# Three placements changed in a gated-scan, linear-attention and fp8 feed-forward kernel: a chunk's norm at the start, group norm's sums in the middle, relu and rounding at the end

## The chip, the cores and the metric

The kernel runs on one core of a Trainium2 chip. The metric is device time in microseconds (us) for one execution, taken as the median of several. The five engines of the core are TensorE (PE, with its weight loads shown apart as PEld), VectorE (DVE), ScalarE (ACT), GpSimd (POOL) and SyncE (SP), which here only issues DMAs. The whole kernel is ordered by hand ("manual schedule"): the order in which the source emits instructions for an engine is the order in which that engine is given them, and engines meet at semaphores.

## The reference

Four images of 64 x 64 pixels with 96 channels go through two layers. Cut to what matters:

```python
# layer 0: x = x + conv(gn(x)); gn is a group norm over 32 groups of 3 channels, per image
xn = layernorm(gn(x)) * gamma + beta                  # per pixel
proj = xn @ W_in + b_in                               # value u, gate g, delta d, and A, B, C (96 x 16 each)
# over the 4096 pixels of an image, one after the other:
h = d * (A * h) + d * (B * u)
y = sigmoid(g) * sum(C * h, axis=states)
x = x + (y @ W_out + b_out)
# layer 1
t = t + attn(ln(t))     # linear attention (no softmax), so K^T V can be folded into one matrix per image
t = t + ffn(ln(t))      # two linear layers, inputs and weights rounded to fp8 (5 exponent bits, 2 mantissa bits),
                        # results rounded to fp16, relu between them
```

The recurrence over pixels is one scan instruction of VectorE per tile. Group norm needs the mean and variance of a whole image before its first pixel can be normed, so the kernel computes them for image b+1 while it scans image b.

## The kernel before

Each image is cut into 8 chunks of 512 pixels, each chunk into 12 tiles (4 groups of states by 3 groups of channels). A tile is one **step**; there are 384 steps. In every step each of the three projections takes three matmuls of 512 columns, and the loop over steps emits, in this order:

```python
for s in range(min(steps), START):      # START = 6; steps 0 to 5 of the scan are planned apart
    call(s)
for s in range(START, K):               # K = 384
    tiles[s + 3].b_proj(); tiles[s + 3].b_copy()      # PE -> bank B (one bank), ACT copies it out
    tiles[s + 1].a_proj()                             # PE -> bank A (two banks)
    tiles[s].c_proj()                                 # PE -> bank C or D
    tiles[s - 1].keep()                               # ACT
    tiles[s + 2].b_mul()                              # POOL
    if tiles[s - 1].on_pool: tiles[s - 1].c_mul_pool()
    tiles[s].scan()                                   # DVE
    tiles[s + 1].a_mul()                              # DVE
    if not tiles[s].on_pool: tiles[s].c_mul()         # DVE
    call(s)                                           # everything else that a table puts at this step
    if tiles[s].on_pool: tiles[s].c_copy()            # ACT
```

`call(s)` emits what the table `AT` puts at step s. Numbers are relative to the first step of a chunk:

```python
AT = {
    "load_x": -39, "centre": -25, "scale": -24, "stats": -22, "rstd": -22, "apply": -21,
    "transpose": -14, "affine": -13, "upper": -13, "low": -12, ...
    "stats_f": 26, "rstd_f": 27, "apply_f": 29, "transpose_f": 30, "quant_in": 31, ...
    "sums": -31,
}
```

The norm of a chunk ahead of its projections is the class `Front`: `centre` and `scale` (POOL, two passes over 128 x 384), `stats` (DVE), `rstd` (POOL, four small operations) and `apply` (ACT, writes tile z), then transposes and projections. The first two chunks are normed in a planned start of their own. For the third chunk (first step 24) the table gives centre -1, scale 0, stats 2, rstd 2, apply 3: all below START, so the first of the two loops above emits all of them at once, after the planned work and ahead of step 6.

Group norm's sums of the next image, one call per chunk of that image:

```python
def sums(self, n):
    self.transpose(n, "M", "gx")                       # PE: four transposes into a bank of ring M (three banks)
    for k, fn in enumerate((AF.Identity, AF.Square)):  # ACT: two passes, each adding up along its rows
        nc.scalar.activation(self.ps, self.ps, fn, bias=self.c if k == 0 else 0.0,
                             accum_out=self.s[:, k, n : n + 1])
...
when = [s0 + AT["sums"] + NT * n for n in range(NCH)]  # one call in 12 steps
if b == 1:
    when = [8, 15, 22, 29, 36, 43, 50, 57]             # the second image: one in 7 steps
```

After the last step a planner orders what is left: feed-forward work of the last three chunks of image 2 and of all eight of image 3. It takes jobs with an engine, an estimated cost and predecessors, and searches orders at random (`end.tries`):

```python
def round_hidden(m):  nc.scalar.copy(v["h16"][:, m, :], v["h", m])              # PSUM -> fp16, 128 x 512
def relu_vector(m):   nc.vector.tensor_scalar(h, h, b1_q[:, m : m + 1], 0.0, ALU.add, ALU.max)
def quant():          nc.scalar.activation(v["hq"], v["h16"], AF.Copy, saturate=False)   # fp16 -> fp8, 128 x 1536
...
for m in range(NK):                                                             # NK = 3
    h = job("PE", 0.24, hidden, m, ...)
    c = job("ACT", 0.57, round_hidden, m, ...)
    r.append(job("DVE", 0.5, relu_vector, m, after=[c]))
a = job("ACT", 1.5, quant, after=r, ...)
a = job("PE", 0.5, project_out, after=[a], ...)
```

Of the kernel before, what the change touches and what calls it, by code (L numbers as in the profile page):

```python
# [13 lines left out]
AF = mybir.ActivationFunctionType  # L14
ALU = mybir.AluOpType
# [24 lines left out]
AT = {  # L40

    "load_x": -39, "centre": -25, "scale": -24, "stats": -22, "rstd": -22, "apply": -21,
    "transpose": -14, "affine": -13, "upper": -13, "low": -12, "proj_d": -9, "d_out": -9,
    "proj_u": -9, "du_out": -9, "write": -9, "read": -6, "proj_gate": -3, "gate_out": -1,

    "gather1": 7, "gather2": 11, "gather3": 14,

    "state_sum": 18, "gated": 18, "project_out": 19, "residual": 19, "stats_a": 20,
# [5 lines left out]
    "hidden2": 38, "relu2": 38, "project_f": 40, "round_out": 40, "bias_out": 40, "total": 46,  # L54
    "store": 51,

    "sums": -31,
}
ON_POOL = (0, 2, 7, 8)
XBUFS = 15  # L60
# [3 lines left out]
def conv_attn_hybrid_kernel(  # L64
# [19 lines left out]
    nc = tc.nc  # L84
# [21 lines left out]
    def sb(tag, shape, dtype, name):  # L106
        pool = big if tag in ("x", "gx", "z", "rep") else work
        return pool.tile(shape, dtype, tag=tag, name=name, bufs=BUFS[tag])
# [123 lines left out]
    b1_q = const.tile([P, NK], F32, name="b1_q")  # L232
# [294 lines left out]
    def at(step, fn, *args):  # L527
        steps.setdefault(step, []).append((fn, args))
# [4 lines left out]
    class GroupNorm:  # L533
# [34 lines left out]

        def sums(self, n):
            self.transpose(n, "M", "gx")  # L570
            for k, fn in enumerate((AF.Identity, AF.Square)):
                nc.scalar.activation(
                    self.ps, self.ps, fn, bias=self.c if k == 0 else 0.0,
                    accum_out=self.s[:, k, n : n + 1],
                )
# [51 lines left out]
    def group_norm(b, s0):  # L627
        q = {}

        def make():  # L630
            q["g"] = GroupNorm(b)
            q["g"].first()

        def call(name, *args):
            getattr(q["g"], name)(*args)

        when = [s0 + AT["sums"] + NT * n for n in range(NCH)]
        if b == 1:  # L640
            when = [8, 15, 22, 29, 36, 43, 50, 57]
        if b > 1:
            at(when[0] - 7, load_gx, b, 0)
        at(when[0] - 2, make)
        for n in range(NCH):
            if n:
                at(max(when[n] - 7, when[n - 1]), load_gx, b, n)
            at(when[n], call, "sums", n)
        for n, name in ((1, "moments"), (2, "mean"), (4, "root"), (6, "diagonal"), (8, "spread"),
                        (8, "spread_out")):  # L650
            at(when[-1] + n, call, name)


    split, rep, gate = {}, {}, {}
# [104 lines left out]
    def front(b, i, s0, f=None):  # L759
        if f is None:  # L760
            f = Front(b, i)
            plan = [
                ("centre", f.centre, nc.gpsimd), ("scale", f.scale, nc.gpsimd), ("stats", f.stats),
                ("rstd", f.ln.rstd), ("apply", f.apply), ("transpose", f.transpose),
                ("affine", f.affine), ("upper", f.upper), ("low", f.low), ("proj_d", f.proj, 2),
                ("d_out", f.d_out), ("proj_u", f.proj, 0), ("du_out", f.du_out),
                ("write", f.write), ("read", f.read),
            ]
            if (b, i) not in xt:
                plan.insert(0, ("load_x", load_x, b, i))  # L770
        else:
            plan = []
        plan += [("proj_gate", f.proj, 1), ("gate_out", f.gate_out)]
        for name, fn, *args in plan:
            at(s0 + AT[name], fn, *args)

    state = {}
    chs = {}
# [86 lines left out]
    def state_sum(g, last=None, first=None):  # L865
# [5 lines left out]
        for cg in range(NCG):  # L871
# [10 lines left out]
    end = Plan(  # L882
        {"A": 2, "B": 1, "C": 1, "M": 3, "yg": 1, "xal": 2, "xat": 1, "xn8": 2, "bu": 5, "h": 3, "rep": 2,
         "xs": 2, "xl": 2, "z": 2, "mv": 4},
        {"ACT": 0.5, "DVE": 2.5, "POOL": 1.5},
    )
    end.last = {}
    end.tries = 800

    def place(plan, s0):  # L890

# [161 lines left out]
    def ffn(b, i, s0):  # L1053
        nm = f"{b}_{i}"
        v, ln = {}, LayerNorm(1e-5, f"f_{nm}")
# [56 lines left out]
                v["h16"] = sb("rep", [P, NK, TC], F16, f"h16_{nm}")  # L1112
            nc.scalar.copy(v["h16"][:, m, :], v["h", m])  # L1113

        def relu_vector(m):
            h = v["h16"][:, m, :]
            nc.vector.tensor_scalar(h, h, b1_q[:, m : m + 1], 0.0, ALU.add, ALU.max)  # L1117

        def quant():
            v["hq"] = sb("bu", [P, NK, TC], F8, f"hq_{nm}")  # L1120
            nc.scalar.activation(v["hq"], v["h16"], AF.Copy, saturate=False)  # L1121

        def project_out():
            ps = v["ps"] = bank("A" if phase["end"] else "M", [P, J, C], f"y2_ps_{nm}")
# [56 lines left out]
        def job(engine, cost, fn, *args, **kw):  # L1181
            return None if fn in done else end.job(engine, cost, fn, *args, **kw)

        a = job("SP", 0.5, fetch, after=[end.last.get((b, i))], late=2.5, take=[f"xal:{nm}"])
        a = job("PE", 0.46, attention, after=[a, b == B - 1 and end.last["r"]], take=[f"A:a{nm}"],
                free=[f"xal:{nm}"])
        a = job("DVE", 0.57, residual, after=[a], free=[f"A:a{nm}"])
        a = job("DVE", 1.6, ln.stats, t, after=[a], take=[f"mv:{nm}"])
        a = job("POOL", 1.3 if vector else 1.8, ln.rstd, not vector, after=[a])
        a = job("DVE" if vector else "ACT", 1.9 if vector else 1.8, apply, after=[a], take=[f"xn8:{nm}"], free=[f"mv:{nm}"])  # L1190
        a = job("PE", 0.45, transpose, after=[a], take=[f"C:{nm}"], free=[f"xn8:{nm}"])
        a = job("ACT", 0.6, quant_in, after=[a], take=[f"h:{nm}"], free=[f"C:{nm}"])
        if hidden not in done:
            r, h, c = [], None, None
            for m in range(NK):
                h = job("PE", 0.24, hidden, m, after=[a, h], take=[f"M:{m}{nm}"],
                        free=[f"h:{nm}"] if m == 2 else [])
                c = job("ACT", 0.57, round_hidden, m, after=[h, c],
                        take=[f"rep:{nm}"] if m == 0 else [], free=[f"M:{m}{nm}"])
                r.append(job("DVE", 0.5, relu_vector, m, after=[c]))  # L1200
            a = job("ACT", 1.5, quant, after=r, take=[f"bu:q{nm}"], free=[f"rep:{nm}"])
        a = job("PE", 0.5, project_out, after=[a], take=[f"A:y{nm}"], free=[f"bu:q{nm}"])
        a = job(*(("ACT", 0.48) if vector else ("DVE", 0.56)), round_out, after=[a],
                take=[f"xs:{nm}"], free=[f"A:y{nm}"])
        last_two = b == B - 1 and i > NCH - 3
        a = job(*(("DVE", 0.6) if last_two else ("POOL", 0.95)), bias_out, after=[a], take=[f"xl:{nm}"], free=[f"xs:{nm}"])
        a = job(*(("DVE", 0.8) if last_two else ("POOL", 0.92)), total, after=[a], take=[f"z:{nm}"], free=[f"xl:{nm}"])
# [4 lines left out]
    START = 6  # L1212
# [153 lines left out]
    for b in range(B):  # L1366
        for i in range(NCH):
            g = b * NCH + i
            s0 = g * NT
            if g:  # L1370
                front(b, i, s0, second if g == 1 else None)
            for sh in range(1, NSH):
                if g < N - 1 or sh == 1:
                    at(s0 + AT[f"gather{sh}"], gather, g, sh)
            at(s0 + NT, tail, b, i)
            s = s0 + NCH * NT
            first = min(24, AT["fetch"])
            at(s + first if b == B - 1 else min(s + first, K - 4), ffn, b, i, s)
        if b + 1 < B:
            group_norm(b + 1, b * NCH * NT)  # L1380
        s = (b + 1) * NCH * NT
        at(s if s == K else s + AT["gram_add"] - NT + 1, attn_matrix, b, s)
# [82 lines left out]
```

## Time and profile before

| | before |
|---|---|
| time, median of 3 | 1202.92 us (1202.42 to 1204.29) |
| span of the profiled execution | 1199.1 us |
| busy PE / PEld | 1148.7 us (96%) / 876.9 us (73%) |
| busy DVE | 1110.0 us (93%) |
| busy POOL | 1032.2 us (86%) |
| busy ACT | 817.8 us (68%) |
| DMA | mean 152 GB/s |

Rows such as `L824 DVE TENSOR_TENSOR_SCAN h<-Aps,state,bu` name the source line, the engine, the operation and the tiles that it writes and reads. In a timeline each row begins with its start and its duration in us, and a bracket at the end tells how long the engine had been idle before it and which instruction ended that idle time. Lines that matter here: L269 is every projection matmul (told apart by the bank it writes: Bps, Aps, Cps, Dps), L805 is `b_copy`, L808 `b_mul`, L817 `a_mul`, L824 `scan`, L396 `apply` on ACT (tile z in layer 0's norm, xn ahead of the feed-forward), L543 the transposes of group norm's sums, L572 the sums, L910 the gating that follows a chunk's sum over states, L920 the residual after layer 0's output projection (o_ps), L1085 the transposes of xn, L1113 `round_hidden`, L1117 `relu_vector`, L1121 `quant`, L403 `apply` on DVE, L1142 and L1149 the last two additions of the feed-forward.

The ends of matmuls are modelled, so two matmuls in a row overlap on the page; their starts tell the rate. In the stretch from 803 to 837 us the 512-column projections start 0.23 us apart.

### The profile page before, as it was taken

The page shows a single profiled execution, that of the slowest core. Times are in us where ns is not written, and L with a number is a line of the kernel's source. Part 1 is how long each engine was busy: PE and PEld are TensorE (multiplying, and loading weights), DVE is VectorE, ACT ScalarE, POOL GpSimd, SP SyncE. Part 2 cuts the span into 40 slices and gives each one's busy share as a digit, 9 for nine tenths or more (in the row PEclk, how much of TensorE's full clock was granted, in tenths as well). Part 3 has the DMA queues.
Part 4 walks back from the last instruction along what each step waited for, and adds up shares of the span by engine and source line. Part 5 has one row for each costly group of instructions (what it writes and reads, how often), then busy time and mean ns, then how long its engine had stood idle before and what let it go on. Part 6 is the DMA issues. An engine that isn't in the chain of part 4 may idle for free. (4 is left out here: it accounts for less than half of the span.)

```text
span 1199.1 us, 19211 instructions
## 1 busy us (share of the span) xinstructions
PE 1148.7 (96%) x5899; PEld 876.9 (73%) x5899; DVE 1110.0 (93%) x2091; ACT 817.8 (68%) x1828; POOL 1032.2 (86%) x1178
## 2 busy tenths in 40 slices
PE   7799999999999999999999999999999999999885
PEld 6567777677777777777777777777777777777663
DVE  6789999999999999999999999999999999999865
ACT  5465666565555777777777777777777777776476
POOL 3877888888988898999998899999999999988564
PEclk8989999999999999999999999999999999999987
DMA  7566776877776766776677677677776787667221
GB/s 187 127 127 145 153 162 159 175 156 160 168 162 150 162 156 146 175 175 156 155 158 164 152 176 177 135 160 160 163 174 153 163 181 159 151 146 165 60 74 46
DMA packets 104288, 182.12 MB, mean 152 GB/s; under 512 B 42637, under 2 KB 50769, under 8 KB 104186
## 3 DMA queue, kind: packets, MB, share of 16 engines
q1 hardware_dynamic: 90060, 106.96, 37.0%
q0 software_dynamic: 13536, 73.93, 31.0%
q8 instruction: 46, 0.75, 0.3%
q14 instruction: 56, 0.46, 0.1%
q10 hardware_dynamic: 590, 0.02, 0.0%
HBM read 69.12 MB, written 24.77 MB: 78 GB/s over the span
## 5 line engine op out<-in xcount | busy, mean ns | idle before, releaser
L808 POOL TENSOR_TENSOR bu<-bu,rep 128x512 f32<-128x512 f32 x384 | 512.3, 1342 | 53.6 <-ACT state L834 38.5
L824 DVE TENSOR_TENSOR_SCAN h<-Aps,state,bu 128x512 f32<-128x512 f32 x336 | 426.0, 1268 | 0.6 <-POOL ch L857 0.5
L805 ACT ACTIVATE bu<-Bps,b_bac 128x512 f32<-128x512 f32 x384 | 262.3, 683 | 188.7 <-PE Bps L269 185.9
L817 DVE SCALAR_TENSOR_TENSOR Aps<-Aps,b_bac,rep 128x512 f32<-128x512 f32 x384 | 281.8, 734 | 12.6 <-PE Aps L269 12.6
L269 PE MATMUL Bps<-xs,w 128*128 128x512 f32 x768 | 268.5, 431 | 16.1 <-ACT bu L805 15.6
L269 PE MATMUL Aps<-xs,w 128*128 128x512 f32 x768 | 242.4, 396 | 1.2 <-DVE h L824 1.1
L857 POOL TENSOR_TENSOR ch<-ch,h 128x512 f32<-128x512 f32 x128 | 172.5, 1348 | 14.1 <-ACT ch L854 10.7
L269 PEld LDWEIGHTS Aps<-xs,w 128*128 128x128 f32 x768 | 143.6, 188 | 38.0 <-DVE h L824 3.7
L269 PEld LDWEIGHTS Bps<-xs,w 128*128 128x128 f32 x768 | 126.5, 191 | 61.1 <-ACT bu L805 26.3
L269 PE MATMUL Aps<-xl,w 128*128 128x512 f32 x384 | 151.9, 396 | 0.0
L269 PE MATMUL Bps<-xl,w 128*128 128x512 f32 x384 | 151.8, 395 | 0.0
L269 PE MATMUL Dps<-xs,w 128*128 128x512 f32 x384 | 121.0, 396 | 0.0
L269 PE MATMUL Cps<-xs,w 128*128 128x512 f32 x384 | 120.7, 395 | 0.3 <-ACT ch L854 0.3
L848 DVE SCALAR_TENSOR_TENSOR ch<-Dps,b_bac,h 128x512 f32<-128x512 f32 x160 | 118.6, 741 | 0.8 <-PE Dps L269 0.7
L863 POOL DMA_DIRECT2D ch<-ch x94 | 90.1, 958 | 0.8 <-DMA ch<-ch 0.8
L269 PEld LDWEIGHTS Bps<-xl,w 128*128 128x128 f32 x384 | 72.5, 189 | 17.7
L269 PEld LDWEIGHTS Dps<-xs,w 128*128 128x128 f32 x384 | 72.3, 188 | 17.6
L269 PEld LDWEIGHTS Aps<-xl,w 128*128 128x128 f32 x384 | 72.2, 188 | 17.7
L269 PEld LDWEIGHTS Cps<-xs,w 128*128 128x128 f32 x384 | 71.9, 188 | 17.9 <-ACT ch L854 0.4
L854 ACT ACTIVATE ch<-Cps,b_bac 128x512 f32<-128x512 f32 x96 | 65.8, 685 | 22.9 <-PE Cps L269 22.9
L269 PE MATMUL Dps<-xl,w 128*128 128x512 f32 x192 | 75.8, 395 | 0.0
L269 PE MATMUL Cps<-xl,w 128*128 128x512 f32 x192 | 75.7, 394 | 0.0
(200 smaller groups left out, 2048.2 us busy)
## 6 DMA issues: line engine op xcount, KB each, us to landing
ch<-ch POOLq DMA_DIRECT2D x94, 768.0 KB, 6.6
rep<-ddd SPq DMA_DIRECT2D x124, 384.0 KB, 7.0
ddd<-dd SPq DMA_DIRECT2D x31, 384.0 KB, 3.2
xl<-lo SPq DMA_DIRECT2D x62, 128.0 KB, 2.5
x<-in_x_dram SPq DMA_DIRECT2D x32, 192.0 KB, 2.9
xatd<-xat SPq DMA_DIRECT2D x32, 192.0 KB, 3.6
xal<-xatd SPq DMA_DIRECT2D x32, 192.0 KB, 2.9
out_dram<-o SPq DMA_DIRECT2D x32, 192.0 KB, 2.1
```

Source lines behind the costliest of these rows:

```text
L269: nc.tensor.matmul(ps, lhsT=wt[:, n], rhs=mv, start=(n == 0), stop=(n == 2))
L805: nc.scalar.activation(self.bu, self.b_ps, AF.Identity, bias=self.bias(0))
L808: nc.gpsimd.tensor_tensor(self.bu, self.bu, rep[self.b, self.i][:, 1, self.cg], ALU.mult)
L817: nc.vector.scalar_tensor_tensor(self.a_ps, self.a_ps, self.bias(1), rep[self.b, self.i][:, 0, self.cg], ALU.add, ALU.mult,)
L824: nc.vector.tensor_tensor_scan(self.h, self.a_ps, self.bu, 0.0 if self.i == 0 else state[self.sh, self.cg], ALU.mult, ALU.add,)
L848: nc.vector.scalar_tensor_tensor(self.slot(), self.c_ps, self.bias(2), self.h, ALU.add, ALU.mult)
L854: nc.scalar.activation(self.ch, self.c_ps, AF.Identity, bias=self.bias(2))
L857: nc.gpsimd.tensor_tensor(self.ch, self.ch, self.h, ALU.mult)
L863: nc.gpsimd.dma_start(chs[g, 0], chs.pop((g, sh)), accum_op=ALU.add)
```

## The change

It has three parts. First, the third chunk's norm is not emitted ahead of step 6 but spread over steps 6 to 9. Second, group norm's sums are split: the transposes stay where they were, ACT's two passes come one step later. Third, in the planned end, GpSimd takes the relu of one of three row blocks in chunks of odd number, and the rounding to fp8 in chunks whose number is divisible by four; the random search gets more tries.

```diff
-    "sums": -31,
+    "sums": -31, "sums_out": -30,

         def sums(self, n):
             self.transpose(n, "M", "gx")
+
+        def sums_out(self, n):
             for k, fn in enumerate((AF.Identity, AF.Square)):

             at(when[n], call, "sums", n)
+            at(when[n] + AT["sums_out"] - AT["sums"], call, "sums_out", n)

         plan += [("proj_gate", f.proj, 1), ("gate_out", f.gate_out)]
+        late = {"centre": 0, "scale": 0, "stats": 1, "rstd": 2, "apply": 3}
         for name, fn, *args in plan:
-            at(s0 + AT[name], fn, *args)
+            step = s0 + AT[name]
+            at(max(step, START + late[name]) if name in late else step, fn, *args)

-    end.tries = 800
+    end.tries = 1500

-        def relu_vector(m):
+        def relu_rounded(m, engine):
             h = v["h16"][:, m, :]
-            nc.vector.tensor_scalar(h, h, b1_q[:, m : m + 1], 0.0, ALU.add, ALU.max)
+            engine.tensor_scalar(h, h, b1_q[:, m : m + 1], 0.0, ALU.add, ALU.max)

         def quant():
             v["hq"] = sb("bu", [P, NK, TC], F8, f"hq_{nm}")
-            nc.scalar.activation(v["hq"], v["h16"], AF.Copy, saturate=False)
+            if i % 4:
+                nc.scalar.activation(v["hq"], v["h16"], AF.Copy, saturate=False)
+            else:
+                nc.gpsimd.tensor_copy(v["hq"], v["h16"], saturate=False)

-            r, h, c = [], None, None
+            r, h, c, on_pool = [], None, None, (1,) if i % 2 else ()
             ...
-                r.append(job("DVE", 0.5, relu_vector, m, after=[c]))
-            a = job("ACT", 1.5, quant, after=r, ...)
+                r.append(job(*(("POOL", 1.0) if m in on_pool else ("DVE", 0.45)), relu_rounded, m,
+                             nc.gpsimd if m in on_pool else nc.vector, after=[c]))
+            a = job(*(("ACT", 1.5) if i % 4 else ("POOL", 2.2)), quant, after=r, ...)
```

## The prediction

> **What bounds the kernel now.** I read four views in this order: busy shares over the span, the table of waits, the timelines of the places that the waits point to, and the busy time of the last 75 us.
>
> The shares over forty slices come first: PE 9 almost throughout, DVE 9, ACT 5 to 7, and two weak ends.
>
> ```profile
> PE   7799999999999999999999999999999999999885
> DVE  6789999999999999999999999999999999999865
> ACT  5465666565555777777777777777777777776476
> ```
>
> ACT has slack, so in the middle an operation of ACT matters only if somebody stands behind it. The table of waits says where that is:
>
> ```profile
> ACT gx_ps L572 <- PE gx_ps L543: 25.3, 23, 1.8
> PEld Bps L269 <- ACT bu L805: 26.3, 24, 7.7
> ```
>
> Group norm's sums keep ACT standing 23 times, 1.1 us each, and PE waits for the copy-out of bank B, once for 7.7 us. That one is in the start; the timeline of 47 to 66 us has it:
>
> ```profile
> 59.46 1.54 ACT L396 ACTIVATE z<-z,nmr_c,rstd_c 128x96 f32<-128x96 f32 x4 [8.13 <-POOL nmr_c L384]
> 56.47 0.74 DVE L371 BATCH_NORM_STATS2 st_c<-z 128x6 f32<-128x96 f32 x4 [3.33 <-POOL z L670]
> 64.59 0.76 DVE L817 SCALAR_TENSOR_TENSOR Aps<-Aps,b_bac,rep 128x512 f32<-128x512 f32 x1 [3.58 <-PE Aps L269]
> 61.63 1.22 PE L269 MATMUL Bps<-xs,w 128*128 128x512 f32 x2 [7.44 <-ACT bu L805]
> ```
>
> ACT stands 8.13 us at the third chunk's apply, whose mean and rstd POOL gives only at 59.4. The copy-out behind it is late, bank B is full, PE stops for 7.44 us, and DVE has gaps of 3.33 and 3.58.
>
> For the middle I lay a chunk with sums beside one of the last image, which has the same feed-forward work but no sums:
>
> ```profile
> 423.75 0.65 ACT L572 ACTIVATE gx_ps<-gx_ps,gmc 96x512 f32<-96x512 f32 x1 [1.14 <-PE gx_ps L543]
> 425.14 1.53 ACT L396 ACTIVATE xn<-x,nmr_f,rstd_f 128x96 fp8e5<-128x96 f32 x4
> 425.65 1.30 PE L1085 MATMUL xq_ps<-ident,xn 128*128 128x128 fp8e5 x4
> 428.03 0.69 DVE L910 TENSOR_TENSOR yg<-y_ps,gate 96x512 f32<-96x512 f32 x1 [0.90 <-PE y_ps L872]
> ```
>
> ```profile
> 808.75 1.54 ACT L396 ACTIVATE xn<-x,nmr_f,rstd_f 128x96 fp8e5<-128x96 f32 x4
> 811.39 0.40 PE L1085 MATMUL xq_ps<-ident,xn 128*128 128x128 fp8e5 x4
> 813.30 0.68 DVE L910 TENSOR_TENSOR yg<-y_ps,gate 96x512 f32<-96x512 f32 x1
> ```
>
> With sums, xn is pushed behind them on ACT; PE reaches its transposes at 425.65 and takes 1.30 us for them instead of 0.40, as each waits for a slice of xn. Everything after them on PE is late, and DVE stands 0.90 us ahead of the gating. From one L910 to the next it is 34.87 us in chunks with sums (428.03 to 462.89, 534.71 to 569.59) and 33.48 without (813.30 to 846.78).
>
> The end is ACT's (columns: stretch, length, busy and instructions, clock, DMA):
>
> ```profile
> 1140.00:1186.00 46.00, 38.24 (x70) 0.89 0.23 64
> L1121 ACT ACTIVATE hq<-h 128x1536 fp8e5<-128x1536 f16 x11 | 16.0, 1494 | 0.1
> 1178.22 2.93 DVE L403 TENSOR_SCALAR xn<-x,mv_f,rstd_f 128x96 fp8e5<-128x96 f32 x4
> ```
>
> It is 83% busy between 1140 and 1186, and eleven roundings to fp8 at 1.494 us are 16 us of it.
>
> **What the Trainium skill says.** "Perfetto Trace Analysis", Tensor Engine Instruction: ACT, DVE and GpSimd queues are strictly first in, first out. The trace agrees: a finished bank B stood behind an apply that waited 8.13 us. "GPSIMD Engine Reference", Engine selection: with two inputs GpSimd is about half as fast as VectorE, with one roughly at line rate. The first half shows (128x512 with two inputs, L808, 1342 ns); for one input the trace has only small ones, a cast of 128x128 to fp8 at 289 ns and memsets of 128 and 512 elements at 205 and 520 ns. "SBUF — State Buffer", Who interferes with whom: a VectorE tensor_scalar in a two-port mode and a GpSimd operation lock each other out. That fits the last row above: four L403 take 2.93 us while POOL runs L1142 and L1149 without a break, and 1.04 us elsewhere (1154.72).
>
> **Part 1, the third chunk's norm.** Nothing is removed; five calls move behind steps 6 to 9. I followed the new order with durations from the trace. POOL is busy until 54.34 either way (low parts of the weights). Then, before: centre, scale, 1.14 idle, rstd, and b_mul of tile 8 at 59.38. After: b_mul of tile 8 at once, centre and scale (to 57.6), b_mul of tile 9, a gather's issue (0.9), b_mul of tile 10 and c_mul of tile 7, then rstd, done near 64.1. ACT's apply follows at 64.1 to 65.6, the first sums (now in the same step) to 67.1, the copy-out of tile 13 to 67.8. So PE stops again, for the projection of tile 14, until 67.8. In the profile before, that projection began at 74.11: 6.3 us earlier. DVE agrees: a_mul of tile 12 needs a projection that ends near 69.2, so scan 12 starts near 70.7 where it was 77.16, 6.5 us earlier; from there both orders are the same and DVE has no gap over 0.5 us until 88. I take **6.4 us**. POOL would allow 5.3 us in that stretch (its idle times 1.14, 1.01, 0.15, 1.28 and 1.82 vanish), but it has two tiles of lead on the scan.
>
> **Part 2, the sums.** Of the eleven chunks from 388.85 to 740.08 with sums and feed-forward, ten show the full loss of 34.87 - 33.48 = 1.39 us; the first shows a third. With the passes a step later, xn follows at once on ACT (from 422.6), ends near 424.1, and PE's transposes no longer wait. The passes run when ACT otherwise stands (2.76 us idle ahead of the copy-out at 813.72, against 1.5 us for the passes). What stays is the transposes' own time: next matmul 0.35 us after them, and PE is the bound here. Gain 1.39 - 0.35 = 1.04 us, times 10, plus 0.3: **10.7 us**. The chunks without feed-forward (228 to 356 us) run at 31.7 with sums; DVE's own work fills the step there, so nothing. The second image's sums, one in 7 steps: those at 88.37 and 107.19 are followed by PE gaps of 1.45 and 1.53, and a step later they miss apply and share with less: about 2 us back. But the seventh now falls on the step of d_out and apply, the place of the one at 88.37, and the eighth on apply_a: about 1.1 and 0.8 us lost. Net 0.3.
>
> **Part 3, the end.** ACT loses two of eleven roundings, 2 x 1.49 = 3.0 us; DVE loses six relus of about 0.35, off the path. On POOL a one-input pass is an estimate: from 289 ns for 128 elements and (520 - 205)/384 = 0.82 ns for each further one, 0.6 us for a relu and 1.5 us for a rounding, 4 and 3 or more in sum, into 29.9 of 53.1 us busy. ACT is busy 80% of the time from 1140 to the last addition, so 3.0 x 0.8 = 2.4; I take off 0.4 for VectorE operations that meet GpSimd's. A new random order adds spread, not a mean: **2.0 us**.
>
> Sum: 6.4 + 10.7 + 0.3 + 2.0 = 19.4. From 1202.9 that is **1183.5 us**, 1.6% faster.
>
> **Rivals.** (a) The moved norm just moves the stop: rstd stays behind POOL's b_muls, ACT stands at apply as long as before, and PE stops at tile 14 instead of tile 10. For it: ACT still has one apply that waits for POOL. Against it: the stop is met after three more tiles. It would leave 2 us of part 1: 1188. (b) The gain per chunk is the whole 1.39 us or more, if the transposes' 0.35 us hides: DVE waits 0.49 us at L920 in chunks without sums, for PE, which speaks against; 1180. (c) Bank M is held a step longer and PE waits for it. The ring of three next needs that bank at the first h matmul or o_ps, near 815 in the chunk without sums, when the passes have ended near 812.5; I hold it unlikely. It would eat part 2: 1193. (d) In the end GpSimd's roundings lock VectorE out, or the new order is worse on the chip than in its plan: the end gets 2 us longer, 1187. It can also turn out 5 us shorter, 1180.
>
> **Range and chances.** I give part 1 plus or minus 2, part 2 plus or minus 2.5, the second image's sums plus or minus 1.5, the end plus or minus 3; in quadrature 4.7, with both tails of the rivals 1177 to 1190.5 for 8 in 10. A gain of over 2% needs 1178.9, 4.6 us more than my sum: 0.15. Slower by 2% would need a stop that nothing shows: 0.01.
>
> **What would show it.** Right: no PE gap over 4 us between 50 and 70 us, and scan 12 near 70.7; waits of ACT L572 for gx_ps near zero; L1085 at 0.4 us in every chunk; L910 to L910 at 33.8 where it was 34.87; new PE gaps near 1 us at the second image's seventh and eighth sums; last addition 2 us nearer to the last step. Wrong: a stop of 6 us or more near 64 us (rival a), 34.9 unchanged with waits for ring M (c), ACT idle more than before after 1140 while DVE rows stretch beside GpSimd's (d).

## The result and the profile after

| | before | after |
|---|---|---|
| time, median | 1202.67 us (1202.33 to 1204.29) | 1184.09 us (1180.64 to 1186.38) |
| ratio to before, 95% interval | | 0.984 (0.9815 to 0.9866) |
| span of the profiled execution | 1199.1 us | 1182.5 us |

Predicted were 1183.5 us, so the sum holds. The question is whether its terms do. The shares over forty slices of the kernel after come first, the rows that were shown of before:

```profile
PE   7999999999999999999999999999999999999985
DVE  6889999899999999999999999999999999999875
ACT  5556656556556777777877787777777777776475
```

PE's second slice (30 to 59 us) went from 7 to 9: the long stop is out of it. The table of waits of after (total, times, longest):

```profile
ACT bu L811 <- PE Bps L269: 194.4, 171, 2.9
...
PEld Bps L269 <- ACT bu L811: 15.0, 19, 2.8
PEld Bps L269 <- ACT gx_ps L574: 12.6, 15, 0.8
```

The row of ACT standing at the sums for their transposes (25.3 us before) is gone. Lines have moved by a few in the kernel after: L811 is `b_copy`, L814 `b_mul`, L823 `a_mul`, L830 the scan, L854 VectorE's `c_mul`, L863 GpSimd's, L860 `c_copy`, L574 the sums, L916 the gating, L1091 the transposes of xn, L1123 the relu, L1128 and L1130 the rounding on ACT and on GpSimd. PE's longest wait for the copy-out of bank B is 2.8 us where it was 7.7. The last row looks like a new wait for the sums, but isn't: the weight-load unit is idle for 0.84 us each time because PE streams six matmuls of y_ps meanwhile (419.18 to 420.24 in the chunk below), and the sums only happen to end then; before, the same 0.8 us stood under another name. The start's timeline, rows of ACT, PE and DVE:

```profile
63.66 1.54 ACT L396 ACTIVATE z<-z,nmr_c,rstd_c 128x96 f32<-128x96 f32 x4 [4.09 <-POOL nmr_c L384]
63.39 0.51 PE L269 MATMUL Dps<-xl,w 128*128 128x512 f32 x1 [2.76 <-DMA w<-w]
63.93 0.75 DVE L854 SCALAR_TENSOR_TENSOR ch<-Dps,b_bac,h 128x512 f32<-128x512 f32 x1 [2.13 <-PE Dps L269]
67.55 0.76 DVE L823 SCALAR_TENSOR_TENSOR Aps<-Aps,b_bac,rep 128x512 f32<-128x512 f32 x1 [1.74 <-PE Aps L269]
```

ACT stands 4.09 us at the third chunk's apply instead of 8.13. PE still stops, for 2.76 us, but at something the prediction does not have: half a weight that arrives by DMA. A chunk of the middle, with sums, after:

```profile
415.77 1.54 ACT L396 ACTIVATE xn<-x,nmr_f,rstd_f 128x96 fp8e5<-128x96 f32 x4
418.32 0.65 ACT L574 ACTIVATE gx_ps<-gx_ps,gmc 96x512 f32<-96x512 f32 x1
418.86 0.40 PE L1091 MATMUL xq_ps<-ident,xn 128*128 128x128 fp8e5 x4
420.33 0.69 DVE L916 TENSOR_TENSOR yg<-y_ps,gate 96x512 f32<-96x512 f32 x1
```

xn goes ahead of the sums, PE takes 0.40 us for the transposes instead of 1.30, and DVE no longer stands ahead of the gating. From one L916 to the next it is 33.8 to 34.2 us in seven of these eleven chunks (33.3 to 35.7 in the others). The end, first the 46 us that correspond to those shown of before (columns: stretch, length, busy and instructions of PE, PEld, DVE, ACT, POOL, then clock, DMA share, GB/s), then the relus and roundings (count: shortest, median, longest in ns), then VectorE beside GpSimd:

```profile
1124.00:1170.00 46.00, 38.12 (x264) 27.91 (x260) 35.42 (x121) 36.09 (x68) 37.49 (x46) 0.81 0.23 65
```

```profile
L1123 DVE TENSOR_SCALAR h<-h,b_q x27: 340/348/1416, 1116.2 to 1169.0; 128x512 f16<-128x512 f16 x27
L1128 ACT ACTIVATE hq<-h x9: 1467/1483/1502, 1122.0 to 1171.3; 128x1536 fp8e5<-128x1536 f16 x9
L1123 POOL TENSOR_SCALAR h<-h,b_q x6: 2003/2018/2382, 1113.6 to 1167.5; 128x512 f16<-128x512 f16 x6
L1130 POOL CAST hq<-h x2: 1472/1564/1655, 1146.5 to 1164.9; 128x1536 fp8e5<-128x1536 f16 x2
```

```profile
1145.81 3.72 DVE L403 TENSOR_SCALAR xn<-x,mv_f,rstd_f 128x96 fp8e5<-128x96 f32 x4
```

ACT is 2.15 us less busy than before (38.24 to 36.09). A rounding on GpSimd takes 1.5 us, as estimated; a relu takes 2.0 us, not 0.6.

To place the gain, I number the scans by step and compare the time between scans of the two kernels (start of a scan to start of a later scan, from the timelines):

| steps | before | after | gain | predicted |
|---|---|---|---|---|
| start to scan 4 | 46.09 | 45.30 | 0.8 | 0, the same instructions |
| 4 to 12 | 31.07 | 26.18 | 4.9 | 6.4 (first part) |
| 12 to 17 | 13.30 | 13.31 | 0.0 | 0 |
| 17 to 48 | 86.13 | 83.37 | 2.8 | 2 (second image's sums) |
| 48 to 60 | 33.92 | 35.09 | -1.2 | -1.9 (its seventh and eighth) |
| 60 to 66 | 17.74 | 19.18 | -1.4 | 0 |
| 66 to 120 | 144.85 | 144.82 | 0.0 | 0 |
| 120 to 383 | 752.03 | 741.98 | 10.1 | 10.7 (sums, chunks with feed-forward) |
| scan 383 to the end | 73.97 | 73.27 | 0.7 | 2.0 (third part) |

The gains add up to 16.6 us, the difference of the two profiled spans; the medians differ by 18.6. So some 2 us of this table belong to the two executions and not to the kernels. Which rows those are was the first thing to find out.

### The profile page after: what moved, and what is told of

The parts are those of the page before. It is cut to its first block, busy times and chain, and to the rows that moved or that the text cites. A ratio compares the mean times of both kernels' runs of the same rounds, so it can differ in the third digit from the quotient of the medians.

```text
span 1182.5 us, 19167 instructions
## 1 busy us (share of the span) xinstructions
PE 1141.2 (97%) x5884; PEld 874.5 (74%) x5884; DVE 1110.0 (94%) x2085; ACT 816.7 (69%) x1826; POOL 1047.2 (89%) x1186
## 5 line engine op out<-in xcount | busy, mean ns | idle before, releaser
L814 POOL TENSOR_TENSOR bu<-bu,rep 128x512 f32<-128x512 f32 x384 | 513.4, 1346 | 44.6 <-ACT state L840 31.8
L830 DVE TENSOR_TENSOR_SCAN h<-Aps,state,bu 128x512 f32<-128x512 f32 x336 | 426.0, 1268 | 0.7 <-POOL ch L863 0.6
L811 ACT ACTIVATE bu<-Bps,b_bac 128x512 f32<-128x512 f32 x384 | 263.0, 685 | 198.4 <-PE Bps L269 194.4
L823 DVE SCALAR_TENSOR_TENSOR Aps<-Aps,b_bac,rep 128x512 f32<-128x512 f32 x384 | 281.8, 734 | 9.3 <-PE Aps L269 9.3
L863 POOL TENSOR_TENSOR ch<-ch,h 128x512 f32<-128x512 f32 x128 | 173.3, 1354 | 8.9 <-ACT ch L860 4.8
L854 DVE SCALAR_TENSOR_TENSOR ch<-Dps,b_bac,h 128x512 f32<-128x512 f32 x160 | 118.6, 741 | 3.0 <-PE Dps L269 2.8
L860 ACT ACTIVATE ch<-Cps,b_bac 128x512 f32<-128x512 f32 x96 | 66.0, 687 | 24.5 <-PE Cps L269 24.5
```

Source lines behind the costliest of these rows:

```text
L811: nc.scalar.activation(self.bu, self.b_ps, AF.Identity, bias=self.bias(0))
L814: nc.gpsimd.tensor_tensor(self.bu, self.bu, rep[self.b, self.i][:, 1, self.cg], ALU.mult)
L823: nc.vector.scalar_tensor_tensor(self.a_ps, self.a_ps, self.bias(1), rep[self.b, self.i][:, 0, self.cg], ALU.add, ALU.mult,)
L830: nc.vector.tensor_tensor_scan(self.h, self.a_ps, self.bu, 0.0 if self.i == 0 else state[self.sh, self.cg], ALU.mult, ALU.add,)
L854: nc.vector.scalar_tensor_tensor(self.slot(), self.c_ps, self.bias(2), self.h, ALU.add, ALU.mult)
L860: nc.scalar.activation(self.ch, self.c_ps, AF.Identity, bias=self.bias(2))
```

## The experiments

Theory: three independent gains, the first cut short by the DMA and the half clock that follows it, the third by GpSimd's slow relu. Rivals: the parts need each other; the order of the sums matters and not their step; the end's gain is that of another random order.

### Each part alone

```diff
# p1_norm: before, with
+        late = {"centre": 0, "scale": 0, "stats": 1, "rstd": 2, "apply": 3}
-            at(s0 + AT[name], fn, *args)
+            step = s0 + AT[name]
+            at(max(step, START + late[name]) if name in late else step, fn, *args)
# p2_sums: before, with
+    "sums_out": -30,
+        def sums_out(self, n):                 # the two passes, out of sums()
+            at(when[n] + AT["sums_out"] - AT["sums"], call, "sums_out", n)
# p3_end: before, with
-    end.tries = 800
+    end.tries = 1500
+    # relu m = 1 of odd chunks and the rounding of chunks divisible by 4: job("POOL", ...)
```

> The kernel before with the first part alone (third chunk's norm behind steps 6 to 9). The prediction's sum: 6.4 us shorter than before. My reading of the trace after the change: 4.9, because PE's stop no longer ends at ACT's copy-out but at a weight DMA that lands near 63 us. If that is so, this kernel too shows a PE gap of 2 to 3 us near 63 us that ends at a DMA, ACT stands about 4 us at the third chunk's apply, and scan 12 starts 4.9 us earlier relative to scan 4 than before. If instead the 1.5 us are lost because the third chunk's norm and the sums' later pass meet on ACT (rival), this kernel alone gets the whole 6.4.

> The kernel before with the second part alone (sums' two passes a step later). My reading: 10 to 10.5 us shorter than before (ratio near 0.991), all of it in the eleven chunks with sums and feed-forward (34.9 to about 33.9 us per chunk); second image's steps 17 to 66 net within 0.5 us of before; the start's stop of 7.4 us stays whole. Rival: the gain needs the shifted phase that part one brings, then it is under 8 us.

> The kernel before with the third part alone (GpSimd's relus and roundings in the planned end). Prediction: 2.0 us shorter; the trace after shows 0.7 from the last scan to the last addition. I expect 0.5 to 1 us shorter (ratio 0.999 to 1.000), with GpSimd's relu at 2.0 us each and its rounding near 1.5 us. If the prediction's 0.6 us for a relu were a matter of neighbours in the trace after, the relus would be shorter here.

| | time | ratio to before (95%) | in us | steps 4 to 12 | 17 to 48 | 120 to 383 | 383 to end |
|---|---|---|---|---|---|---|---|
| p1_norm | 1197.01 | 0.9958 (0.9942 to 0.9974) | -5.1 | 27.93 | 86.14 | 752.11 | 73.39 |
| p2_sums | 1190.31 | 0.9900 (0.9882 to 0.9917) | -12.0 | 30.72 | 83.36 | 741.88 | 73.31 |
| p3_end | 1199.69 | 0.9975 (0.9966 to 0.9984) | -3.0 | 30.51 | 86.15 | 752.12 | 70.89 |

(In us: the ratio's distance from 1, times 1202.93, the median of before beside these runs.) Together 20.1 us, where all three at once give 19.2 (0.016 x 1202.93; interval 16.1 to 22.3): within the intervals the parts add up. Each part works in its own stretch and leaves those of the others alone, as the columns show. p2_sums puts 10.1 us into the chunks with feed-forward and 2.8 into steps 17 to 48, without the first part's shift. p3_end shows 3.1 us in the end, four times what I had read from the trace after. p1_norm has the expected stop at a DMA, but longer, 4.04 us and not 2 to 3, and gains only 2.6 to 3.1 us between scans 4 and 12, not the 4.9 that I expected of it:

```profile
65.46 0.80 PE L269 MATMUL Dps<-xl,w 128*128 128x512 f32 x1 [4.04 <-DMA w<-w]
66.05 1.05 PE L269 MATMUL dug_ps<-xs,w_dug 128*96 128x512 f32 x2
```

The second row is the hint to the next finding: two matmuls in 1.05 us, where relu_dve below shows the same two in 0.63.

### Executions of the same instructions, side by side

Six of the kernels have the start of after, instruction for instruction (after, and relu_dve, image2, no_pool, round800 and no_pool800 below). Between scans 4 and 12 they took 26.18, 24.96, 26.31, 27.05, 26.14 and 27.33 us. The clock of PE in after (first fence) and in relu_dve (second), in two stretches of 1 us after the DMA stop, reads like this:

```profile
64.00:65.00 1.00, 1.00 (x4) 0.75 (x3) 1.00 (x2) 1.00 (x4) 1.00 (x2) 0.52 1.11 227
65.00:66.00 1.00, 1.00 (x3) 0.74 (x3) 0.81 (x1) 0.97 (x4) 1.00 (x1) 0.50 1.14 233
```

```profile
64.60:65.60 1.00, 1.00 (x6) 0.80 (x5) 1.00 (x2) 1.00 (x4) 1.00 (x2) 1.00 0.99 203
65.60:66.60 1.00, 1.00 (x6) 0.81 (x5) 0.80 (x1) 0.97 (x4) 1.00 (x1) 1.00 1.11 227
```

PE is busy throughout in both; in after it does three or four matmuls per us, in relu_dve six, since the granted clock (third number from the end) is 0.50 in one and 1.00 in the other. In both a stop of PE went ahead, of 2.76 and 2.74 us:

```profile
63.39 0.51 PE L269 MATMUL Dps<-xl,w 128*128 128x512 f32 x1 [2.76 <-DMA w<-w]
63.73 0.79 PE L269 MATMUL dug_ps<-xs,w_dug 128*96 128x512 f32 x2
```

```profile
63.98 0.50 PE L269 MATMUL Dps<-xl,w 128*128 128x512 f32 x1 [2.74 <-DMA w<-w]
64.31 0.63 PE L269 MATMUL dug_ps<-xs,w_dug 128*96 128x512 f32 x2
```

Read us by us, the clock of every run is 1.00 or 0.50, and what a stretch of half clock loses (one minus the clock, summed) comes as 1.7 us or a multiple, so in units of 3.4 us of half clock. The start after PE's stop has none in relu_dve (24.96 us), one in after, image2 and round800 (26.18, 26.31, 26.14), two in no_pool and no_pool800 (27.05, 27.33): about 1.2 us each. The Trainium skill, "TensorE: Matmul & The Clock Gate", Part 1: The HAM clock gate, describes this: an activity monitor halves the matmul clock after an idle window of about 3.4 us that runs freely, so that its phase differs from run to run. The halves and the length agree with the trace. The size of the gap doesn't: here half clock followed stops shorter than the window, of 2.76 to 2.93 us in these starts, and in read_last (below) of 0.61 and 1.65 us around four transposes that took 1.39 us. Step 65 shows best that it need not follow, where every one of the fourteen profiled executions has a PE stop of 2.35 to 2.81 us: five of them had no half clock and took 3.79 to 3.81 us for the step (before and p1_norm among them), nine had it and took 4.57 to 5.36 (p3_end, whose instructions there are those of before, and after). So the row "60 to 66: -1.4" of the table is no effect of the change.

The start of before has half clock too, which has to be kept in mind when its 31.07 us are the measure. From the end of its stop of 7.44 us, at 61.63, to 66.5 us its clock is 0.50. The last pair of matmuls before that ends, and the first after it:

```profile
65.64 1.05 PE L269 MATMUL Bps<-xs,w 128*128 128x512 f32 x2
66.77 0.62 PE L269 MATMUL Aps<-xs,w 128*128 128x512 f32 x2
```

p3_end, with the same instructions, and p2_sums have half clock behind that stop as well (30.51 and 30.72 us). No execution shows the start of before at full clock.

### The order of the sums or their step: same_step

```diff
-            at(when[n] + AT["sums_out"] - AT["sums"], call, "sums_out", n)
+            at(when[n] - 1, lambda n=n: at(when[n], call, "sums_out", n))   # same step, emitted last in it
```

> The kernel after, but the sums' two passes stay in the step of their transposes and are only put behind everything else that the table has for that step (so behind xn on ACT). Theory: what counts in the chunks with feed-forward is that xn goes ahead of the passes, not the step itself; these chunks keep their gain of about 1 us each and this kernel is within 2 us of after, with the second image's steps 17 to 66 about as before. Rival: the passes need the later step, because PE's transposes for them are not done; then ACT stands at the passes again and some 5 to 10 us of the gain are lost.

1185.23 us, ratio to before 0.9856 (0.9841 to 0.987). Steps 120 to 383 take 741.82 us, as good as after's 741.98: in the chunks with feed-forward the whole 10.1 us come from xn being ahead of the passes on ACT, and nothing from the later step. The timeline of same_step:

```profile
417.73 1.54 ACT L396 ACTIVATE xn<-x,nmr_f,rstd_f 128x96 fp8e5<-128x96 f32 x4
419.18 0.63 ACT L574 ACTIVATE gx_ps<-gx_ps,gmc 96x512 f32<-96x512 f32 x1
```

The passes follow xn at once, with no bracket: the transposes are long done. In these chunks the rival falls. Where no xn goes ahead, ACT does stand at the passes again, 10 times of 24 as the table of waits of same_step has it:

```profile
ACT gx_ps L574 <- PE gx_ps L543: 10.7, 10, 1.8
```

In the chunks without feed-forward that costs nothing (66 to 120 take 144.82 us, as in after). In the second image the step does count: 17 to 48 take 85.38 us here, 83.37 in after and 86.13 before; 0.75 us of the gain is order, 2.0 is the step.

### The second image's seventh and eighth sums: image2

```diff
-            at(when[n] + AT["sums_out"] - AT["sums"], call, "sums_out", n)
+            at(when[n] + (0 if b == 1 and n > 5 else 1), call, "sums_out", n)
```

> The kernel after, with the passes of the second image's seventh and eighth sums back in their own step. Theory: the gain of steps 17 to 48 (2.7 us) stays and the loss of steps 48 to 66 (2.6 us) goes: 2.6 us shorter than after (ratio to after near 0.998). Rival: the loss of steps 48 to 66 is due to where the earlier sums moved, not to these two; then no change.

1181.47 us, ratio 0.9827 (0.981 to 0.9843). Steps 17 to 48 keep their gain (83.38), 48 to 60 take 33.72 instead of 35.09: 1.4 us, not 2.6, because the rest of what I had read as a loss is step 65's clock. PE's stop that the prediction named is the one that goes; after had

```profile
181.66 0.73 PE L269 MATMUL Bps<-xs,w 128*128 128x512 f32 x2 [1.38 <-ACT bu L811]
```

and image2 has no PE gap over 0.4 us in that stretch. All of it is the seventh: the loss sits in steps 53 and 55 (3.27 and 2.96 us, with 2.49 and 2.36 in image2); the eighth's step 58 is 2.75 in after and 2.76 in image2, although PE has a gap of 0.95 us there in after.

### The DMA of the start: read_last and norm_early

SyncE issues that weight's two halves (w<-w) behind the four reads of the second chunk (rep<-ddd). Rows of its queue, in after and then in read_last:

```profile
53.23 1.99 SPq L754 DMA_DIRECT2D rep<-ddd  x4
55.26 0.60 SPq L262 DMA_DIRECT2D w<-w  x1
55.90 0.61 SPq L263 DMA_DIRECT2D w<-w  x1
```

```profile
53.03 0.60 SPq L262 DMA_DIRECT2D w<-w  x1
53.73 0.59 SPq L263 DMA_DIRECT2D w<-w  x1
54.44 2.00 SPq L754 DMA_DIRECT2D rep<-ddd  x4
```

```diff
# read_last: after, with
-        job("SP", 1.8, second.read, after=[a])
+        job("SP", 1.8, second.read, after=[a, w[2, NSH - 1]])
# norm_early: read_last, with
-        late = {"centre": 0, "scale": 0, "stats": 1, "rstd": 2, "apply": 3}
+        late = {"centre": 0, "scale": 0, "stats": 1, "rstd": 1, "apply": 2}
```

> The kernel after, with the planned start's four reads of the second chunk issued behind the last copies of weights instead of ahead of them on SyncE's queue. Theory: the weight half that ended PE's stop of 2.76 us near 63 us waits behind those reads; it lands at least 2 us earlier, PE starts tile 14's projections sooner, and the scans from 12 on come 1.5 to 2.5 us earlier than in after. Rival 1: the reads are then late and the second chunk stops VectorE: slower by 1 us or more. Rival 2: the copy-out of bank B behind ACT's apply (near 66 us) is the next stop, and under 1 us is gained.

> The kernel after with two edits in the start: the second chunk's reads behind the last weights on SyncE's queue (as in read_last), and GpSimd's rstd and ACT's apply of the third chunk one step earlier. Theory: with the weights in time the next stop is ACT's, which stands at apply until rstd ends near 63.5 us because rstd stands behind two more passes of GpSimd; one step earlier it ends 2.5 us sooner, PE has no stop over 1 us between 55 and 70, no stretch of half clock follows, and scans from 12 on come 2 to 3.5 us earlier (counted from scan 4) than in after. Rival: GpSimd's own passes for the tiles come later by what rstd takes (1.8 us) and VectorE waits for them instead: under 1 us is gained.

read_last: 1184.29 us, ratio 0.9848 (0.9833 to 0.9862). The wait for the DMA is gone and scan 10 comes 2.25 us earlier than in after (17.05 instead of 19.30 from scan 4). But from there to scan 12 it takes 9.12 us instead of 6.88, and the sum is 26.17 where after has 26.18. Both executions have one stretch of half clock. The next stop takes it all:

```profile
64.09 1.39 PE L684 MATMUL xnt_ps<-ident,z 128*96 128x128 f32 x4 [0.61 <-ACT z L396]
67.12 0.73 PE L269 MATMUL Bps<-xs,w 128*128 128x512 f32 x2 [1.65 <-ACT bu L811]
```

The third chunk's apply on ACT ends near 65 either way, and the transposes, the sums and the copy-out of bank B stand behind it: rival 2 of that run, and the prediction's own stop. norm_early attacks it: 1183.5 us, ratio 0.984 (0.9824 to 0.9857). apply starts 2.5 us earlier, as expected, if it is counted from scan 4 (15.90 us behind it; 18.36 in after), but ACT still stands for it:

```profile
62.20 1.54 ACT L396 ACTIVATE z<-z,nmr_c,rstd_c 128x96 f32<-128x96 f32 x4 [4.20 <-POOL nmr_c L384]
63.65 0.67 ACT L860 ACTIVATE ch<-Cps,b_bac 128x512 f32<-128x512 f32 x1
64.22 0.67 ACT L811 ACTIVATE bu<-Bps,b_bac 128x512 f32<-128x512 f32 x1
```

because two copies that were ahead of it are now behind. PE stops 2.41 us for the last of these and VectorE 1.2 us for GpSimd. Scans 4 to 12 take 24.25 us without half clock, 0.7 less than relu_dve's 24.96, also without; the same start in best (below), with one stretch, takes 25.79, 0.4 less than after's. Under 1 us, as its rival had it.

### The end: relu_dve, no_pool, round800, no_pool800

```diff
# relu_dve, after with all relus on VectorE
-            r, h, c, on_pool = [], None, None, (1,) if i % 2 else ()
+            r, h, c, on_pool = [], None, None, ()
# no_pool: relu_dve with all roundings on ACT
-            a = job(*(("ACT", 1.5) if i % 4 else ("POOL", 2.2)), quant, after=r, ...)
+            a = job("ACT", 1.5, quant, after=r, ...)
# round800, no_pool800: relu_dve and no_pool with
-    end.tries = 1500
+    end.tries = 800
```

> The kernel after, with all relus of the end back on VectorE; GpSimd keeps the two roundings. Theory: six relus of 2.0 us on GpSimd (0.34 on VectorE) stand in front of ACT's roundings and stretch VectorE beside them, and cost 1 to 2 us: the end from the last scan to the last addition gets 1 to 2 us shorter than after. Rival: ACT's 83% busy time bounds the end and the relus are hidden: within 0.5 us, either way. A third: VectorE's relus cost it as much as they free: the end is longer.

> The kernel after, with the end's relus on VectorE and all roundings on ACT (so only the longer search of orders and the cheaper estimate for VectorE are left of the third part). Theory: the two roundings moved to GpSimd bring about 2 us and its relus cost about 1 to 2; without both the end is within 1 us of before's, 0.7 us longer than after's. Rival: the new order alone is what the end gained: no difference to after, or shorter.

> The kernel after, all relus of the end on VectorE, the two roundings on GpSimd, and the search cut to 800 orders: another order of the same jobs as in relu_dve. It tells the chosen order from the placement. If the two roundings on GpSimd are what shortens the end, it takes 70 to 72 us from the last scan to the end again (relu_dve 70.7, GpSimd's whole third part 70.9 to 73.3); if the order decides, it can be anywhere from 70 to 76.

> The kernel after, with all relus on VectorE, all roundings on ACT, and the search cut to 800 orders: another order of the same jobs as in no_pool. If ACT's two further roundings are what lengthens the end, it takes 73 to 76 us from the last scan to the end (before 73.3 to 74.0, no_pool 75.4); if no_pool only had a poor order, it is near 71.

Two things had to be told apart from the placement, the clock and the order. The clock: six executions have the end of after, three that of before.

| order of the end | granted clock of the 68 us after the last scan: time from it to the end |
|---|---|
| third part's (p3_end, image2, same_step, after, read_last, norm_early) | 0.96: 70.89; 0.92: 71.27; 0.87: 72.66; 0.85: 73.27; 0.85: 73.20; 0.85: 73.27 |
| before's (p2_sums, p1_norm, before) | 0.97: 73.31; 0.95: 73.39; 0.90: 73.97 |
| relus on VectorE, two roundings on GpSimd (relu_dve, best; round800) | 0.92: 70.70, 0.91: 70.73; 0.95: 69.57 |
| nothing on GpSimd (no_pool; no_pool800) | 0.95: 75.41; 0.90: 70.35 |

These are the rows of after and of p3_end behind the first line (PE's busy time differs by 4.5 us, ACT's and POOL's by 0.1):

```profile
1109.00:1177.00 68.00, 53.56 (x382) 37.83 (x382) 47.20 (x166) 47.18 (x84) 49.24 (x60) 0.85 0.23 65
```

```profile
1125.50:1193.50 68.00, 49.06 (x381) 33.16 (x380) 46.34 (x166) 47.19 (x84) 49.37 (x60) 0.96 0.24 67
```

At 0.95 to 0.97 the third part's end is 2.5 us shorter than before's (70.89, one execution, against 73.35, the mean of two). The 0.7 us of the first table compare an execution at 0.85 with one at 0.90.

The order: the last two lines of the table hold two orders each of the same jobs on the same engines. Without GpSimd they are 5.1 us apart, and the better, 70.35 at 0.90, is shorter than any of the third part's own order. That one, no_pool800, says most: its end has every job on the engine that it has in before, and as many tries. Only the planner's estimate for VectorE's relu differs (0.45 for 0.5), and with it the order and the number of matmuls that the planner puts into PE's gaps (43 for 56; nothing reads their results). The 68 us after the last scan in before, then in no_pool800:

```profile
1125.20:1193.20 68.00, 55.98 (x403) 39.34 (x403) 45.74 (x172) 49.17 (x86) 34.42 (x52) 0.90 0.22 61
```

```profile
1111.60:1179.60 68.00, 52.82 (x390) 36.58 (x390) 45.29 (x172) 49.68 (x86) 34.48 (x52) 0.90 0.24 67
```

At the same clock it is 3.6 us shorter than before's end (73.97), with nothing moved to GpSimd; the whole third part brings 2.5. The theory of no_pool, that it would land within 1 us of before's end, missed at 75.4; its result alone (1186.93 us, ratio 0.9872, 0.9858 to 0.9887) would have said that the two roundings on GpSimd are worth several us. no_pool800 (1183.0 us, 0.9835, 0.9817 to 0.9854) takes that back. The relus on VectorE come out at 69.6 to 70.7 in two orders, less than the third part's 70.9 to 73.3, which fits the theory that GpSimd's relus cost 1 to 2 us; but times do not separate them (relu_dve 1183.14 us, 0.9834, 0.9812 to 0.9855; round800 1181.93 us, 0.983, 0.9811 to 0.9849; after 0.984), and the spread between orders is as large. Open stays how much of the third part's 2.5 us is GpSimd's help and how much the luck of the order; two orders of each kind are too few to tell. A longer search did not help by itself: with 1500 tries the end is longer than with 800 in both pairs (75.41 and 70.35, 70.70 and 69.57). The third part's own jobs were not searched with 800.

### All together: best

```diff
# after, with the edits of norm_early, image2 and relu_dve
```

> norm_early, the second image's seventh and eighth sums undelayed (as in image2), and all relus of the end on VectorE (as in relu_dve). If the three gains add up: 2.5 us of the start, 1.3 to 2.8 of the second image, 0 to 1.5 of the end, so 1177 to 1180 us, 0.4 to 0.6% under after and 2.0% or more under before. Rival: what the start gains is lost at the next stop (as in read_last), then 1181 to 1182.

1180.96 us, ratio 0.9823 (0.9806 to 0.984), the shortest of the study, but not the 1177 to 1180 that were expected. Its start (25.79) and steps 48 to 60 (33.71) are those of norm_early and image2, its end (70.73) that of relu_dve: the gains stand side by side, but they are smaller than expected (0.4, 1.4 and what the end's order gives), and against after's 0.984 (0.9815 to 0.9866) the difference is within the intervals.

## Why the prediction was right, term by term

The total, 19.4 predicted and 18.6 to 19.2 measured, is right. Of the four mechanisms two are as predicted (the sums, in both places), the first is in part, and the fourth is not shown. The sizes:

- **First part, 6.4: mis-sized.** Scans 4 to 12 give 4.9 in the profiled pair and 4.5 as the mean of the six executions with after's start against the two with before's (26.33 against 30.79; before and p3_end). What failed is the step "PE stops again, for the projection of tile 14, until 67.8": it took every weight as there, and it ran the matmuls behind the stop at full rate. PE stopped earlier, 2.76 us for a weight that SyncE issues behind four reads. By itself that cost nothing (read_last against after, one execution and one stretch of half clock each), because the stop named in the prediction stands behind it and would have taken the same time: ACT's apply began at 63.66 where I had 64.1, its copy-out ended at 67.15 where I had 67.8, in an execution that was 0.8 us earlier from scan 4 on. What did cost is the half clock after the stop, 1.2 us a stretch, which the sum had nowhere. The one execution without it gained 31.07 - 24.96 = 6.1 us, but that is no like for like: 4.9 us of before's matmuls ran at half clock. At full clock in both the part would bring some 4.4 us; this is an estimate, from 4.9 x 0.5 = 2.4 us of clock lost in before and 1.2 us of time for each 1.7 us lost. So the forecast held a start at full clock (tile 14's six matmuls from 67.8 to 69.2) against a record with half clock in it.

  Alone, the part is worth 5.1 us by the times (3.1 to 7.0) but 2.6 to 3.1 in scans 4 to 12. The profiled execution of p1_norm has two stretches of half clock, and its weight came 1.2 us later than in after (19.3 us behind scan 4, 18.1 in after); against the two executions of after's start with two stretches (27.05 and 27.33) its 27.93 us are 0.6 to 0.9 more. Whether it lacks some help of the second part, or this is the one execution, is not shown.
- **Rival (a), the stop only moves: half true.** ACT's wait at apply was halved (8.13 to 4.09 us), and PE's stop moved, to the DMA (7.44 to 2.76).
- **Second part in the chunks with feed-forward, 10.7: right,** 10.1 us in every run with the sums behind xn. 34.87 - 33.48 less 0.35 us per chunk was the right difference; the gating is 33.8 to 34.2 us apart where 33.8 was predicted. Rivals (b) (the whole 1.39) and (c) (waits for ring M) fall: the chunks kept about 0.4, and no wait for the ring appears. The reason given was the right one, and same_step shows it to be the only one: the order on ACT, not the step. Chunks without feed-forward: 0.0 of 0.
- **Second image's sums, net 0.3: mis-sized, mechanism right.** (The terms 2, 1.1 and 0.8 give 0.1, not 0.3.) The early sums gained 2.8 where I had 2, the seventh lost 1.4 where I had 1.1, and the eighth's 0.8 did not come: PE has the gap (0.95) but no scan waits for it. Net 1.4.
- **Third part, 2.0: right in size, cause not shown.** 3.0 us by the times of the part alone (1.9 to 4.1), 2.5 at like clock. The term "0.6 us for a relu" was wrong by a factor of three (2.0 us), as I took arithmetic with two operations on fp16 to cost per element what memsets cost; the cast, 1.5 us, was right. And the step from ACT being busy 80% of the time to 3.0 x 0.8 = 2.4 is not shown: with all eleven roundings on ACT (no_pool800) ACT is busy 49.68 us of the 68, as in before (49.17), and the end is 3.6 us shorter than before's at the same clock. So it was not ACT's work that kept before's end from being shorter. That a new order "adds spread, not a mean" was right, but the spread, 5.1 us in one pair, is larger than the term. (Of the eleven roundings only eight, some 12 us, lie in the 46 us shown, not all 16 us.)

So the terms measured are 4.5 + 10.1 + 1.4 + 2.5 = 18.5 us. The 1.5 to 2 us too much in the first part and 0.6 in the chunks met the 1.1 too little in the second image's sums and the 0.5 in the end; that the sum is right to 1 us with terms that are off by 2 is luck. (Two sums of the working are off by a rounding: POOL's idle times add up to 5.4 us, not 5.3, and the quadrature gives 4.6, not 4.7. Nothing hangs on them.)

## What to carry to other kernels

On an engine that works in order, look at what an instruction stands in front of. Here, to put group norm's passes behind xn, in the same step, was worth 10 us, and the later step nothing in those chunks. When one stop is removed, list every wait behind it before booking its length: here a DMA and an apply each stood ready to take the same microseconds, and to remove the DMA alone gained nothing. Before a difference of 1 or 2 us between two traces is explained, compare stretches in which both kernels run the same instructions; they differed by as much, and the trace that a forecast starts from has its own half clock. And where a search orders the work, try a second order of the same jobs before the gain is put down to a placement: here two of them were 5.1 us apart.

## What the runs showed of the hardware

- A stop of PE of 2.35 to 2.81 us can be followed by 3.4 us of half clock, and need not be: at step 65 it was in nine of fourteen executions. A matmul pair then takes 1.05 us instead of 0.63. Between scans 120 and 383, where no execution has a stretch of half clock, the eleven runs with xn ahead of the sums agree within 0.2 us in 742; in the start and the end the same instructions spread over 2.4 us.
- GpSimd does a tensor_scalar with two operations on 128 x 512 fp16 in 2.0 us, VectorE in 0.34, and GpSimd a cast of three times the elements (128 x 1536, fp16 to fp8) in 1.5 us: what GpSimd is given matters more than how much. VectorE's four L403 beside it took 3.72 us in after; elsewhere in the same end (1136.12) they took 1.02.
